# Separate PSUM tiles for the halves of the last TensorE conv tile, and one warm-up product fewer

## The chip, the cores and the metric

The kernel runs on one core of one Trainium2 chip. The metric is device time in microseconds (us) of one execution. Before the change it is 2915.72 us, the median of three runs (2914.89 to 2915.89).

## The reference

The input `x` is 16 images of 384 channels and 32 by 32 pixels, fp32. Two residual layers follow one another; each normalises in 32 groups of 12 channels first (`_gn`).

```python
# layer 0: attention over the 1024 pixels of an image, 8 heads of 48
x = x + _L0_conv_ref(_gn(x), L0_conv_w_qkv, L0_conv_w_proj, L0_conv_b_proj)
# layer 1: depthwise 7x7 convolution, weights made symmetric under rotation
x = x + _L1_conv_ref(_gn(x), L1_conv_weight)
```

`_L0_conv_ref` makes q, k and v with one product each, takes a softmax over 1024 keys, sums v with it and projects. `_L1_conv_ref` averages the weight with its three rotations by 90 degrees and convolves every channel with its own 49 taps.

## The kernel before

**Tiling.** An image is held as three tiles (k = 0, 1, 2) of 128 channels by 1024 pixels. `HALF` is 512 pixels, 16 of the 32 image rows. Heads are worked on in pairs. For a pair and eight blocks of keys, TensorE (PE) makes scores (`s_step`, L474), ScalarE (ACT) exponentiates them out of PSUM (L482), and PE sums v with them (`av_step`, L490).

**The start.** Image 0 is needed before anything else can run. While it is loaded, PE multiplies a tile of ones into a PSUM tile that nobody reads (`fill`, L1145). Then `groups_on_pe` makes the group means on PE with two short sets of products on masks (`average`, L313); between their results it calls `between`, which here is `fill(fills.popleft(), 2 * P)`: two products of 256 columns, then four (`fills = deque((2, 4))`). After the last set VectorE (DVE) and GpSimd (POOL) finish the scale (L332, L334, L335), and DVE, ACT and DVE normalise the three tiles of `x` (L341, L345, L341). The first product of q and k (`qk_step`, L423) is behind the fills in PE's queue.

**The convolution.** Most tiles are convolved on DVE, one `scalar_tensor_tensor` over the tile for each tap (`conv_tap`, L621). For three tiles, `PE_TILES` = (14, 2), (15, 2), (15, 1), PE does it (`conv_on_pe`, L729): each half of a tile is 14 taps (13 for the first tile) by four groups of 32 channels, 128 rows deep. A tile has one PSUM tile of two banks, `[P, 2, HALF]`, for both halves, from the pool `ps_s` with its three buffers. When a tile is finished, ACT copies it out (`conv_on_pe_end`, L744) and a transfer adds it to the residual. The last tile is instead added by DVE, half by half, and each half goes to the output at once (`conv_on_pe_half`, L752 and L753: half 0 by POOL's queue, half 1 by SP's).

**The last tile on DVE.** Tile (15, 0), `LONE`, has its 7 taps in the middle column done by ACT and added up in a tile `sum3` by POOL's transfers (L914). DVE does the other 42 taps in turns into two sums, the tile itself (`x` in the trace) and `sum2` (`sum` in the trace). Then it adds `sum3` to `sum2` (L888) and `sum2` to the tile in two halves (L894), each with an output transfer (L895, SP's and ACT's queues).

**The order.** Each engine works through its queue in the order in which the Python code emits instructions. A planner sets that order: `clock` is a model of PE's time, `vclock` one of DVE's. `conv_piece` emits seven taps of PE's convolution and adds 6.2 to `clock`; `catch_up(clock)` then emits DVE's work until `vclock` gets there, at `(950 + 128) / 955` = 1.129 for a tap of the last tile. Between taps it emits what `after(wait, cost, f)` has put on a list, as soon as `vclock` has reached the due time, which is `wait` behind the later of the two clocks at the call. Both halves of the last tile are put there with `after(6.0, 0.7, ...)`. A last tile half has two pieces, so 12.4 of `clock`.

**PSUM.** `ps_s` has three buffers of two banks. `ps_o` has two buffers of one bank (tag `acc`), which hold the sums of `av_step` and, in the last stage, the sums of the softmax (`ps_sum`) and the group means (`ps_st`).

Of the kernel before, what the change touches and what calls it, by code (L numbers as in the profile page):

```python
# [10 lines left out]
F32 = mybir.dt.float32  # L11
I32 = mybir.dt.int32
AF = mybir.ActivationFunctionType
ALU = mybir.AluOpType
AX = mybir.AxisListType

P = 128
# [27 lines left out]
def kernel(  # L45
# [25 lines left out]
    nc = tc.nc  # L71

    B, C, H, W = x.shape
# [5 lines left out]
    HALF = N // 2  # L79
# [30 lines left out]
    def run(general):  # L110
        tag = "g" if general else "f"
        with ExitStack() as stack:
# [3 lines left out]
            def pool(name, bufs, **kw):  # L116
                return stack.enter_context(tc.tile_pool(name=f"{name}_{tag}", bufs=bufs, **kw))
# [13 lines left out]
            ps_o = pool("ps_o", 2, space=bass.MemoryType.PSUM)  # L131

            def psum(name):
                return ps_s.tile([P, 2, HALF], F32, tag="s", name=name)

            xns, x1s, qks, os_, accs, es, xn1s = {}, {}, {}, {}, {}, {}, {}
            xds, shs, pss, mats, psums = {}, {}, {}, {}, {}
            PE_K = [NK - 1, NK - 2]

            PE_TILES = [(B - 2, PE_K[0])] + [(B - 1, k) for k in PE_K]  # L140
# [469 lines left out]
            def region(*ds):  # L610
                return [(slice(max(0, -d), H - max(0, d)), slice(max(0, d), H - max(0, -d))) for d in ds]
# [26 lines left out]
            SH, CH = 4, P // 4  # L638
# [77 lines left out]
            def pe_taps(b, k):  # L716
                return [t for t in PE_TAPS if t != (1, 0) or (b, k) not in ROWS_ONLY]

            def conv_on_pe(b, k, h, first, last):
                if (b, k) not in pss:  # L720
                    pss[b, k] = psum(f"ps_conv_{b}_{k}")
                taps = pe_taps(b, k)
                for n, (d0, dx) in enumerate(taps):
                    if not first <= n < last:
                        continue
                    _, (ox, ix) = region(0, dx)
                    for i in range(SH):
                        src = shs[b, k, h, i // 2][:, i % 2, 0 : ROWS * W]
                        nc.tensor.matmul(  # L729
                            pss[b, k][CH * i : CH * (i + 1), h, :].rearrange(  # L730
                                "p (y x) -> p y x", x=W
                            )[:, :, ox],
                            lhsT=mats[k][:, i, d0 * KS + dx + PAD, :],
                            rhs=src.rearrange("p (y x) -> p y x", x=W)[
                                :, SH * d0 : SH * d0 + H // 2, ix
                            ],
                            start=(n == 0),
                            stop=(n == len(taps) - 1),
                        )

            def conv_on_pe_end(b, k):

                t = tpool.tile([P, N], F32, tag="t", name=f"conv_{b}_{k}")
                nc.scalar.copy(t, flat(pss.pop((b, k))))  # L744
                nc.gpsimd.dma_start(x1s[b, k], t, accum_op=ALU.add)
                conv_end(b, k)

            def conv_on_pe_half(b, k, h):

                c = slice(h * HALF, (h + 1) * HALF)  # L750
                dst = x1s[b, k][:, c]
                nc.vector.tensor_tensor(dst, pss[b, k][:, h, :], dst, ALU.add)  # L752
                (nc.gpsimd, nc.sync)[h].dma_start(  # L753
                    out[b, k * P : (k + 1) * P].rearrange("p h w -> p (h w)")[:, c], dst
                )
# [88 lines left out]
            def now():  # L844
                return vclock if catching else max(clock, vclock)

            def after(wait, cost, f):

                nonlocal count
                count += 1  # L850
                heapq.heappush(later, (now() + wait, count, cost, f))
# [286 lines left out]
            ones = tpool.tile([P, N], F32, tag="t", name="ones_warm")[:, 0:HALF]  # L1138
            nc.vector.memset(ones, 1.0)
            warm = psum("warm")  # L1140
            fills = deque((2, 4))

            def fill(n, cols):
                for i in range(n):
# [60 lines left out]
            def loads(n):  # L1205
                while n and pe_loads and pe_loads[0][0] in xn1s:
                    (b, k), h, a = pe_loads.popleft()
                    conv_load(b, k, h, a)
                    n -= 1

            def conv_piece():
                nonlocal clock
                b, k, h, first, last = pe_conv.popleft()
                while (b, k, h, 1) not in shs and pe_loads:
                    loads(1)
                conv_on_pe(b, k, h, first, last)
                clock += 6.2 * (last - first) / KS
                if last == len(pe_taps(b, k)):
                    loads(2)
                    if (b, k) == PE_TILES[-1]:  # L1220
                        after(6.0, 0.7, lambda: conv_on_pe_half(b, k, h))
                    elif h == 1:
                        after(6.0, 1.2, lambda: conv_on_pe_end(b, k))

# [30 lines left out]
            def fast_end(b):  # L1255
                assert not applies
                for key in ("sum2", "sum3"):
                    late[key] = opool.tile([P, N], F32, tag="o", name=key)
                nc.gpsimd.memset(late["sum3"][:, N - W :], 0.0)

                x1_stats[b].groups_on_pe(late["masks"], tap, conv_piece)
                conv_piece()
                x1_chains(b, x1_stats[b])
# [7 lines left out]
            for b, n0, size in [  # L1271
# [27 lines left out]
                for n in range(n0, n0 + size):  # L1299
                    av_step(n)  # L1300
                    u, h, i = n // (2 * NT), n // NT % 2, n % NT
# [39 lines left out]


            conv_piece()
            fast_end(B - 1)
            clock += 7.0
            vclock = clock
            after(4.0, 1.2, check_vector)
            while later or chains or active or pe_conv:
# [6 lines left out]
                catch_up(clock)  # L1355

    run(False)
    redo = nc.values_load(again[0:1, 0:1], min_val=0, max_val=2 * P)
    with tc.If(redo > 0):
        run(True)  # L1360
# [43 lines left out]
```

## Time and profile before

| | |
|---|---|
| time, median of three runs | 2915.72 us |
| the profiled execution's own time | 2915.74 us |
| its span in the trace | 2913.9 us |
| PE busy | 2898.2 us (99%) |
| DVE busy | 2573.5 us (88%) |
| ACT busy | 1450.9 us (50%) |
| POOL busy | 258.0 us (9%) |
| mean granted clock of PE | 0.997 of full speed |

Times in the trace are counted from the start of the span. The 1.8 us between span and time lie outside the trace. A PE product in fp32 is two records in the trace, each with a weight load (PEld). DVE's and ACT's starts can lie some 0.08 us before the end of the instruction ahead, so the pitch from start to start is what an instruction takes in a row of others. A line of the timeline may merge several instructions of one kind: start, busy time, engine and line, and the count after an x. Square brackets hold idle time of the engine ahead of it, and what ended it.

### The profile page before, as it was taken

To read this page: it belongs to the slowest core of one execution; us is meant where nothing else is said; L and a number is where in the kernel's file an instruction comes from. 1 tells how busy PE (TensorE), PEld (TensorE's weight loads), DVE (VectorE), ACT (ScalarE), POOL (GpSimd) and SP (SyncE) were. 2 spreads that over 40 slices of the span, in tenths; PEclk is the share of its full clock that TensorE was granted. 3 is DMA by queue.
4 is the path that set the end of the run, shared out by engine and by line. 5 is a ranking of instruction groups with operands and counts; after the bars stand their busy time and mean duration, and the time that the engine had idled before them with its cause. 6 is when DMAs were issued, how large, how long until landed. Compare 5 with 4: busy or idle time off the path is not lost. (4 is left out here: it accounts for less than half of the span.)

```text
span 2913.9 us, 30140 instructions
## 1 busy us (share of the span) xinstructions
PE 2898.2 (99%) x11448; PEld 1168.7 (40%) x11448; DVE 2573.5 (88%) x2567; ACT 1450.9 (50%) x1732; POOL 258.0 (9%) x407
## 2 busy tenths in 40 slices
PE   9999999999999999999999999999999999999998
PEld 5343343433434343343433434343343433434332
DVE  5312998989899898998989899898998989899998
ACT  2545545465453655545465453655545465454531
POOL 3111004010100101000010100101001010100101
PEclk9999999999999999999999999999999999999999
DMA  7432012120312203022120312203012120312326
GB/s 282 133 28 63 16 35 76 35 70 17 67 37 43 70 21 84 16 35 70 35 70 16 66 39 43 70 21 84 16 35 70 33 72 16 64 41 43 98 62 180
DMA packets 73355, 172.84 MB, mean 59 GB/s; under 512 B 30432, under 2 KB 32368, under 8 KB 71664
## 3 DMA queue, kind: packets, MB, share of 16 engines
q0 software_dynamic: 33696, 112.73, 15.4%
q1 hardware_dynamic: 38080, 55.20, 7.8%
q10 hardware_dynamic: 1424, 2.88, 0.4%
q8 instruction: 92, 1.51, 0.2%
q14 instruction: 63, 0.52, 0.1%
HBM read 118.61 MB, written 28.72 MB: 51 GB/s over the span
## 5 line engine op out<-in xcount | busy, mean ns | idle before, releaser
L621 DVE SCALAR_TENSOR_TENSOR x<-xn,wsym,x 128x899 f32<-128x899 f32 (+9 forms) x2177 | 2370.4, 1162 | 139.6 <-ACT xn L345 139.6
L482 ACT ACTIVATE e<-ps_s 128x1024 f32<-128x1024 f32 x1024 | 952.4, 1053 | 54.5 <-PE ps_s L474 51.5
L474 PE MATMUL ps_s<-qk 48*128 48x512 f32 x4096 | 914.8, 596 | 1.4 <-ACT qk L430 1.4
L490 PE MATMUL acc<-e,v 128*64 128x512 f32 x4096 | 907.2, 595 | 0.0
L474 PEld LDWEIGHTS ps_s<-qk 48*128 48x128 f32 x4096 | 375.9, 185 | 536.5 <-ACT e L482 258.8
L490 PEld LDWEIGHTS acc<-e,v 128*64 128x64 f32 x4096 | 283.0, 137 | 608.2 <-issue 599.7
L423 PE MATMUL ps_qk<-x,wqk 128*128 128x512 f32 x1152 | 506.6, 596 | 0.0
L501 ACT COPY o<-acc 128x512 f32<-128x512 f32 x128 | 75.1, 587 | 609.4 <-PE acc L490 609.3
L423 PEld LDWEIGHTS ps_qk<-x,wqk 128*128 128x128 f32 x1152 | 216.8, 190 | 286.5 <-issue 286.3
L449 PE MATMUL ps_v<-wv,x 128*128 128x384 f32 x768 | 252.0, 488 | 0.0
L543 PE MATMUL ps_proj<-o,wp 128*128 128x512 f32 x540 | 234.2, 592 | 0.0
L430 ACT COPY qk<-ps_qk 128x1024 f32<-128x1024 f32 x96 | 96.7, 1009 | 254.0 <-PE ps_qk L423 254.0
L558 POOL DMA_DIRECT2D x<-in_x x45 | 39.3, 873 | 1794.7 <-ACT x L551 1421.0
L449 PEld LDWEIGHTS ps_v<-wv,x 128*128 128x128 f32 x768 | 144.6, 190 | 109.6 <-ACT e L482 12.1
L543 PEld LDWEIGHTS ps_proj<-o,wp 128*128 128x128 f32 x540 | 102.6, 190 | 125.9 <-issue 119.8
L458 ACT COPY v<-ps_v 128x384 f32<-128x384 f32 x128 | 55.1, 483 | 185.6 <-PE ps_v L449 185.6
L551 ACT ACTIVATE x<-ps_proj,bp 128x1024 f32<-128x1024 f32 x45 | 50.1, 1113 | 182.7 <-PE ps_proj L543 182.7
L526 DVE TENSOR_TENSOR o<-o,inv 128x1024 f32<-128x1024 f32 x63 | 76.8, 1219 | 68.0 <-DMA inv<-inv 62.6
L345 ACT ACTIVATE xn<-x,sc_x 128x1024 f32<-128x1024 f32 x47 | 54.9, 1230 | 90.1 <-DMA sc_x<-gr_x 66.9
L368 DVE BATCH_NORM_STATS2 bs_all<-xs 128x6 f32<-128x512 f32 x84 | 52.1, 683 | 17.7 <-DMA xs<-in_x 17.7
L729 PE MATMUL ps_conv<-sh,mat 128*32 128x464 f32 (+3 forms) x656 | 67.3, 569 | 0.0
L439 POOL DMA_DIRECT2D qk<-qk x96 | 47.3, 526 | 117.4 <-ACT qk L430 116.4
(135 smaller groups left out, 551.2 us busy)
## 6 DMA issues: line engine op xcount, KB each, us to landing
x<-in_x POOLq DMA_DIRECT2D x90, 512.0 KB, 5.6
inv<-inv SPq DMA_DIRECT2D x126, 256.0 KB
out<-x POOLq DMA_DIRECT2D x46, 512.0 KB, 3.9
xs<-in_x POOLq DMA_DIRECT2D x42, 512.0 KB, 6.5
qk<-qk POOLq DMA_DIRECT2D x96, 128.0 KB, 5.9
o<-o SPq DMA_DIRECT2D x90, 64.0 KB
sh<-xd SPq DMA_DIRECT2D x32, 160.0 KB
x<-in_x SPq DMA_DIRECT2D x6, 512.0 KB
```

Source lines behind the costliest of these rows:

```text
L423: nc.tensor.matmul(ps[:, h, :], lhsT=wqk[:, k, s, t, :], rhs=xns[b][:, k, h * HALF : (h + 1) * HALF], start=(k == 0), stop=(k == NK - 1),)
L430: nc.scalar.copy(halves(qks[u][:, s, :]), ps)
L449: nc.tensor.matmul(ps[:, j, 0:C], lhsT=xns[b][:, k, t * P : (t + 1) * P], rhs=wv[:, k, :], start=(k == 0), stop=(k == NK - 1),)
L458: nc.scalar.copy(dst.rearrange("p (h d) -> p h d", d=D + 1)[:, :, 0:D], ps[:, j, 0:C].rearrange("p (h d) -> p h d", d=D),)
L474: nc.tensor.matmul(ps[:, j, :], lhsT=qks[u][r, 1, i * P : (i + 1) * P], rhs=qks[u][r, 0, h * HALF : (h + 1) * HALF], start=True, stop=True,)
L482: nc.scalar.activation(es[n], ps, AF.Exp, scale=SCALE)
L490: nc.tensor.matmul(accs[u, h][64 * j : 64 * j + 64, :], lhsT=v_of(u, i, j), rhs=e[:, j, :], start=(i == 0), stop=(i == NT - 1),)
L501: nc.scalar.copy(os_[u][:, h * HALF : (h + 1) * HALF], accs.pop((u, h)))
L526: nc.vector.tensor_tensor(os_[u], os_[u], invs.pop(u), ALU.mult)
L543: nc.tensor.matmul(ps[:, h, :], lhsT=wp[:, t, o * P : (o + 1) * P], rhs=os_[NP * b + t][:, h * HALF : (h + 1) * HALF], start=(t == 0), sto ...
L621: nc.vector.scalar_tensor_tensor(acc, xn1s[b, k].rearrange("p (h w) -> p h w", w=W)[:, iy, ix], wsym[:, k, dy + PAD, dx + PAD : dx + PAD + 1],
L729: nc.tensor.matmul(pss[b, k][CH * i : CH * (i + 1), h, :].rearrange("p (y x) -> p y x", x=W)[:, :, ox], lhsT=mats[k][:, i, d0 * KS + dx + ...
```

## The change

1. In `conv_on_pe`, the last tile of `PE_TILES`, (15, 1), gets a PSUM tile of one bank for each half, from the pool `ps_o`. The other two tiles keep their tile of two banks.
2. `conv_on_pe_half` reads the half's own tile.
3. The halves' addition is put on the planner's list with `after(2.0, ...)` in place of `after(6.0, ...)`.
4. The second set of warm-up products ahead of the first q and k has three products in place of four.

```diff
             def conv_on_pe(b, k, h, first, last):
-                if (b, k) not in pss:
-                    pss[b, k] = psum(f"ps_conv_{b}_{k}")
+                if (b, k) == PE_TILES[-1]:
+
+                    if (b, k, h) not in pss:
+                        pss[b, k, h] = ps_o.tile([P, HALF], F32, tag="acc", name=f"ps_conv_{h}")
+                    dst = pss[b, k, h]
+                else:
+                    if (b, k) not in pss:
+                        pss[b, k] = psum(f"ps_conv_{b}_{k}")
+                    dst = pss[b, k][:, h, :]
...
-                            pss[b, k][CH * i : CH * (i + 1), h, :].rearrange(
-                                "p (y x) -> p y x", x=W
-                            )[:, :, ox],
+                            dst[CH * i : CH * (i + 1), :].rearrange("p (y x) -> p y x", x=W)[:, :, ox],
...
-                nc.vector.tensor_tensor(dst, pss[b, k][:, h, :], dst, ALU.add)
+                nc.vector.tensor_tensor(dst, pss.pop((b, k, h)), dst, ALU.add)
...
-            fills = deque((2, 4))
+            fills = deque((2, 3))
...
                     if (b, k) == PE_TILES[-1]:
-                        after(6.0, 0.7, lambda: conv_on_pe_half(b, k, h))
+                        after(2.0, 0.7, lambda: conv_on_pe_half(b, k, h))
```

## The prediction

> **What bounds the kernel now.** I read the page's busy times first, then the timeline of both ends, since the change touches only the first 20 us and the last 20.
>
> ```profile
> PE 2898.2 (99%) x11448; PEld 1168.7 (40%) x11448; DVE 2573.5 (88%) x2567; ACT 1450.9 (50%) x1732; POOL 258.0 (9%) x407
> ```
>
> PE lacks 15.7 us of the span: 1.46 before its first product, 1.10 before the first scores (from the waits of the first 31 us), and 12.8 at the end. Between the ends it has no gap, so what shortens its head moves everything behind it.
>
> The end, in the timeline:
>
> ```profile
> 2855.35 45.72 PE L729 MATMUL ps_conv<-sh,mat 128*32 128x512 f32 x445
> ...
> 2892.41 1.11 DVE L621 SCALAR_TENSOR_TENSOR sum<-xn,wsym,sum 128x870 f32<-128x870 f32 x1
> 2893.44 1.08 DVE L621 SCALAR_TENSOR_TENSOR x<-xn,wsym,x 128x841 f32<-128x841 f32 x1
> 2894.45 1.11 DVE L621 SCALAR_TENSOR_TENSOR sum<-xn,wsym,sum 128x870 f32<-128x870 f32 x1
> 2895.48 1.14 DVE L621 SCALAR_TENSOR_TENSOR x<-xn,wsym,x 128x899 f32<-128x899 f32 x1
> 2898.37 0.56 POOL L631 DMA_DIRECT2D out<-x  x1 [7.06 <-DMA x<-conv]
> 2901.16 0.69 DVE L752 TENSOR_TENSOR x<-ps_conv,x 128x512 f32<-128x512 f32 x1 [4.54 <-PE ps_conv L729]
> 2901.77 1.15 DVE L621 SCALAR_TENSOR_TENSOR sum<-xn,wsym,sum 128x899 f32<-128x899 f32 x1
> 2902.15 0.56 POOL L753 DMA_DIRECT2D out<-x  x1 [3.22 <-DVE x L752]
> ...
> 2905.05 1.23 DVE L888 TENSOR_TENSOR sum<-sum,sum 128x1024 f32<-128x1024 f32 x1
> ...
> 2907.51 0.68 DVE L752 TENSOR_TENSOR x<-ps_conv,x 128x512 f32<-128x512 f32 x1
> ...
> 2908.22 0.36 SPq L753 DMA_DIRECT2D out<-x  x1
> ```
>
> The first L752 adds half 0. DVE stood 4.54 us for it, and started 0.09 us after PE's very last product (2855.35 + 45.72 = 2901.07). When was half 0 done? The last two tiles are 448 records (2 tiles x 2 halves x 14 taps x 4 groups x 2), from 2855.31 to 2901.07: 0.102 us each. Half 1 is the last 112 of them, 11.4 us, so half 0 was complete at about 2889.6, 11.5 us before DVE might read it. The wait is for the whole tile. It also sets the end: from 2901.16 DVE has three taps, L888, L894 twice and half 1, without a gap, and half 1's output leaves at 2908.22; the span ends 5.7 later.
>
> The head, from the timelines of PE and its weight loads, and the table of 1 us stretches (columns: stretch, then busy us of PE, PEld, DVE, ACT, POOL, then PE's clock):
>
> ```profile
> 14.14 3.76 PE L1145 MATMUL warm<-ones_warm 128*128 128x256 f32 x8
> 17.70 4.63 PE L423 MATMUL ps_qk<-x,wqk 128*128 128x512 f32 x8
> ...
> 15.75 1.56 DVE L341 TENSOR_SCALAR x<-x,sc_x 128x1024 f32<-128x1024 f32 x2
> ...
> 18.00:19.00 1.00, 1.00 (x2) 0.37 (x2) 0.48 (x3) 0.00 (x0) 0.99 (x2) 0.50 0.99 393
> 19.00:20.00 1.00, 1.00 (x2) 0.34 (x1) 0.51 (x1) 0.00 (x0) 0.00 (x0) 0.62 0.98 397
> 20.00:21.00 1.00, 1.00 (x4) 0.51 (x3) 1.00 (x3) 0.00 (x0) 0.00 (x0) 1.00 0.64 229
> ```
>
> Four fills take 17.70 - 14.14 = 3.56 us, 0.89 each, at half clock. The first tile of `x` is ready at about 15.75 + 0.82 = 16.57 (the line holds two instructions, median 820 ns), so the fills, not the data, hold the first q and k. The clock becomes full at about 19.8 (0.62 over that stretch is 0.76 us at half and 0.24 at full).
>
> **What the Trainium skill says.** "PSUM — Partial Sum Buffer", Specifications (TRN2): a bank is 2 KiB per partition, 512 fp32 values. So the halves lie in banks of their own already; the summary of rules there asks a reader beside a running product only for another bank. The trace has that pair: ACT reads one score tile while PE writes the next. The 4.54 us is thus nothing that the memory asks for. "TensorE: Matmul & The Clock Gate", What's actually happening: the clock is raised after a busy window of some 3.4 us, and windows run freely. The trace agrees: clock at half from 13 to 19.8 us, two such windows. So one product fewer at 17 us should not delay the raise, as q and k products fill its place. "Perfetto Trace Analysis", Summary: the profiler window per engine type: the record of a transfer from SP's queue leaves out its data movement; hence the 5.7 us from issue to end of span, which I carry over unchanged.
>
> **The change part by part.**
>
> *Own tiles for the halves.* Nothing is computed more: 112 products go to other banks. Half 0 then needs only its own last product, at 2889.6. The two `acc` buffers were last read by DVE for `ps_sum` and for `ps_st` (L335 at 2842.78), 36 us before (15, 1) begins at about 2878.2; so no new wait on PE. `ps_s` loses one user, and no gap of PE there waited for it. Cost 0.
>
> *Where half 0 stands in DVE's queue.* Call C the model clock when half 0's last piece is emitted. Then half 1's first piece is emitted (C + 6.2) and DVE is filled up to there. With 6.0, half 0 was due at C + 6.0, but taps of 1.129 stepped over it, and it came out in the next fill, behind half 1's second piece; the trace agrees, as it stands after the tap of 2895.48. With 2.0 it comes out at the first step at or past C + 2.0, three or four taps earlier: at 2892.41 (taking four), 2.8 us after half 0 is done. No stall; DVE's 4.54 us goes. In numbers: the tap of 2895.48 is 899 wide; such a tap has a pitch of 2902.83 - 2901.77 = 1.06 (the next tap's start from the trace), so half 0 could have started at 2896.54 and did at 2901.16: 4.62 us. The 0.61 of half 0 itself only changes places with four taps.
>
> *Half 1.* It is due 2.0 behind C + 12.4, so at C + 14.4. Half 0 leaves at C + 2.0 to 3.13; with 0.7 for it and nine steps of 1.129 (seven taps, L888, L894) DVE's tile ends at C + 12.9 to 14.0. So half 1 stays last. It would start at 2907.51 - 4.62 = 2902.89, still 1.8 after PE's end; PE does not become the bound.
>
> *What is late next.* L888 moves to 2900.43 and needs `sum3`: its last add was issued at 2889.56 and took 4.3 to land (the list of transfers), 2893.9. Half 0's output on POOL's queue is behind L631, which waits until 2898.37 for the residual of (15, 2): so it leaves at about 2898.9 and not at 2893, 3.2 earlier than before, lands some 2.5 later, as measured, and is 2 us gone before L895 and half 1 send theirs (2902.4 to 2903.6). If POOL's wait grew by some 4 us, they would collide: 256 KB at the 300 GB/s of these stretches, up to 0.9.
>
> *One fill fewer.* PE gets to q and k 0.89 earlier, at 16.81; `x` at 16.57 plus a weight load at half clock (0.34) makes 16.9 the other limit. So 0.8 of q and k products are done earlier, but at half clock: worth 0.4 of full-clock time, as the raise at 19.8 stays. Bounds: 0 (raise already done in a run whose windows lie otherwise, and `x` the limit), 0.45 (0.89 halved). If the raise came one window later it would cost 3.4 x 0.5 = 1.7 (an estimate from the skill's window). I take 0.42. PE carries it to the end without a gap, and DVE's last stage hangs on PE's group means (L313), so the 0.42 adds to the 4.62.
>
> Sum: 5.04. The profiled execution, 2915.74, becomes 2910.7; the median, 2915.72, is the same. That is 0.17%, under the 0.2% (5.8 us) that I take as what a measurement can tell from no change.
>
> **The rivals.**
>
> *A, the gain is 5.0: 2910.7.* As above.
>
> *B, the wait moves along: 2919.4, slower.* If half 0 still waits for PE's last product (PE's progress reported only at the end of an unbroken run of products), the stall begins four taps earlier. Those taps, 2896.54 - 2892.41 = 4.13, then run after 2901: +4.13 - 0.42 = +3.7. It decides at the place where half 0 starts: the end moves by that start less 2897.0. Against it: the ACT copy L744 of (15, 2) ran at 2880.21, soon after that tile's end (2855.31 + 224 x 0.102 = 2878.2), with PE amid (15, 1). For it: this wait's release was PE's very end.
>
> *C, the end is hidden elsewhere: 2913.* DVE ends early, but outputs collide with POOL's late ones, or `sum3` lands late, and half of the 4.6 is lost (2915.7 - 2.3 - 0.4). Speaks for it: L631's wait of 7.06 shows a transfer slow to land; against: the DMA share is near nothing at 2902 to 2903.
>
> *D, the clock falls back: 2912.4.* The tail's 4.62 less 1.7, plus 0.4 at most: the fill was needed for the raise. Against it: PE stays busy without it.
>
> **How the numbers follow.** A 0.85, B 0.04, C 0.06, D 0.05. A's own range is 2910.2 to 2911.6: head 0 to 0.45, and 0.5 either way, as far as the three runs lie apart. D and half of C take the range to 2912.5; below, 2909.7, where a longer wait than the profiled one is taken away. Faster than 2909.9 is the low edge of A, 0.08; slower than 2921.5 nearly nobody, beyond B with a further loss: 0.02; the rest, 0.90, is within 0.2%, though below the time before.
>
> **What would show it.** After the change: L752 of half 0 without a wait, at about 2892, among taps of L621; half 1 at 2902.5, its output at 2903.2, and a span of 2908.9. L1145 with six records from 14.14, the first L423 at 16.8 to 16.95, clock raised near 19.8. I am wrong if L752 has a wait left on PE, if L888 waits for a transfer, or if the last output takes more than 5.7 to the end.

## The result, and the profile after

The kernel with the change takes 2909.64 us, the median of 22 runs (2907.99 to 2912.76). The kernel before takes 2914.93 us (22 runs, 2912.14 to 2917.80, the three that were known among them). The ratio of the two kernels' runs is estimated at 0.9985, with a 95% interval of 0.9979 to 0.9990: 4.4 us less, between 2.9 and 6.1; the two medians lie 5.3 apart. That is a gain, and under the 0.2% that the prediction set as its bound. The forecast was 2910.7, with a range of 2909.7 to 2912.5, so the median lies just below the range. The profiled execution took 2909.63 with a span of 2907.8, so 1.8 us lie outside the trace, as before.

The busy times of the page after the change:

```profile
PE 2896.3 (100%) x11446; PEld 1174.6 (40%) x11446; DVE 2573.6 (89%) x2567; ACT 1451.6 (50%) x1732; POOL 258.4 (9%) x407
```

PE has two records fewer, the one warm-up product. Work is otherwise what it was; what changed is when it is done. The end, in the timeline after the change:

```profile
2852.87 45.98 PE L736 MATMUL ps_conv<-sh,mat 128*32 128x512 f32 x445
...
2889.92 0.67 DVE L757 TENSOR_TENSOR x<-ps_conv,x 128x512 f32<-128x512 f32 x1
2890.53 1.11 DVE L621 SCALAR_TENSOR_TENSOR sum<-xn,wsym,sum 128x870 f32<-128x870 f32 x1
...
2896.36 0.56 POOL L631 DMA_DIRECT2D out<-x  x1 [6.97 <-DMA x<-conv]
2896.91 0.56 POOL L758 DMA_DIRECT2D out<-x  x1
...
2900.40 0.68 DVE L757 TENSOR_TENSOR x<-ps_conv,x 128x512 f32<-128x512 f32 x1
2901.11 0.36 SPq L758 DMA_DIRECT2D out<-x  x1
```

L757 is the line that was L752. Half 0 is added at 2889.92 with no bracket behind it: DVE does not wait for it. It stands before the tap of 870 elements, four taps earlier than before, and 8.9 us before PE's last product ends (2852.87 + 45.98 = 2898.85). Half 1 starts at 2900.40, which is 1.55 after PE's end; before it was 6.44 after.

The head, in the timeline of PE and the table of 1 us stretches (the last columns are PE's clock, the DMA share and GB/s):

```profile
14.19 2.91 PE L1150 MATMUL warm<-ones_warm 128*128 128x256 f32 x6
16.89 5.57 PE L423 MATMUL ps_qk<-x,wqk 128*128 128x512 f32 x12
...
16.00:17.00 1.00, 1.00 (x4) 0.64 (x3) 1.00 (x2) 1.00 (x1) 1.00 (x3) 0.50 0.35 33
17.00:18.00 1.00, 1.00 (x3) 0.42 (x2) 0.97 (x3) 0.04 (x1) 1.00 (x3) 0.80 0.70 209
```

The first product of q and k stands at 16.89, where it was at 17.70. But the clock is full from about 17.4 (0.80 over a stretch is 0.4 us at half and 0.6 at full), not from 19.8.

Put piece by piece, the two profiled executions compare so (us):

| piece | before | after | difference |
|---|---|---|---|
| span's start to the first scores | 30.29 | 28.71 | -1.58 |
| first scores to PE's end | 2870.78 | 2870.14 | -0.64 |
| PE's end to the start of half 1's addition | 6.44 | 1.55 | -4.89 |
| half 1's addition to its output's issue | 0.71 | 0.71 | 0 |
| that issue to the end of the span | 5.7 | 6.7 | +1.0 |
| span | 2913.9 | 2907.8 | -6.1 |

The third row is the change's aim. The last row was not foreseen, and the first is larger than the 0.42 of the prediction. The experiments take these three in turn.

### The profile page after: what moved, and what is told of

It is laid out like the page before. It is cut to its first block, busy times and chain, and to the rows that moved or that the text cites. A ratio compares the mean times of both kernels' runs of the same rounds, so it can differ in the third digit from the quotient of the medians.

```text
span 2907.8 us, 30136 instructions
## 1 busy us (share of the span) xinstructions
PE 2896.3 (100%) x11446; PEld 1174.6 (40%) x11446; DVE 2573.6 (89%) x2567; ACT 1451.6 (50%) x1732; POOL 258.4 (9%) x407
```

## The experiments

A difference in us below is the ratio's distance from 1 times the median of the kernel before in the same group of runs (2914.1 to 2914.7); it has the ratio's interval. Single executions of one kernel spread over some 3 to 6 us here, so an interval is 3 to 5 us wide, and the traces carry what is smaller.

### The tail's parts, one at a time

**Own tiles alone.** The kernel before with the new tiles, `after(6.0, ...)` and four fills left as they were.

```diff
+                if (b, k) == PE_TILES[-1]:
+                    if (b, k, h) not in pss:
+                        pss[b, k, h] = ps_o.tile([P, HALF], F32, tag="acc", name=f"ps_conv_{h}")
+                    dst = pss[b, k, h]
...
-                nc.vector.tensor_tensor(dst, pss[b, k][:, h, :], dst, ALU.add)
+                nc.vector.tensor_tensor(dst, pss.pop((b, k, h)), dst, ALU.add)
```

> Own PSUM tiles for the two halves alone; the halves' due time stays at 6.0 and four warm-up products stay. Theory A (DVE waited for the whole tile, and the tile is all of it): half 0's addition keeps its old place in DVE's order, four taps later than in the changed kernel, and has no wait; half 1's addition starts about 1.8 us after PE's last product, against 6.4 before; the last output leaves 4.6 us earlier, time -4.6 us. Theory B (a wait on PE's last product, whatever the tile): half 0 still waits about 4.5 us, time unchanged. Theory E (the earlier place in DVE's order is what matters): -1 us or less.

Measured: 2911.01, ratio 0.9989 (0.9982 to 0.9996), 3.2 us less. DVE's timeline:

```profile
2894.84 1.14 DVE L621 SCALAR_TENSOR_TENSOR x<-xn,wsym,x 128x899 f32<-128x899 f32 x1
2895.91 0.67 DVE L757 TENSOR_TENSOR x<-ps_conv,x 128x512 f32<-128x512 f32 x1
...
2902.25 0.68 DVE L757 TENSOR_TENSOR x<-ps_conv,x 128x512 f32<-128x512 f32 x1
```

Half 0 stands at its old place, behind the tap of 899, and is added without a wait. PE ended at 2900.44, so half 1 starts 1.81 after it. The tiles alone remove the whole wait.

**The earlier place alone.** The kernel before, shared tile, four fills.

```diff
-                        after(6.0, 0.7, lambda: conv_on_pe_half(b, k, h))
+                        after(2.0, 0.7, lambda: conv_on_pe_half(b, k, h))
```

> Only the halves' due time goes from 6.0 to 2.0; both halves stay in one PSUM tile, four warm-up products. DVE then has half 0's addition four taps earlier, in program order between the two pieces of half 1. Theory A (the wait goes by the tile): it waits about 3.0 us, for the last product of half 1's first piece, 5.7 us after half 0 is done, and PE's second piece has to wait for this read, a gap of about 0.75 us on PE; half 1's addition starts 4.1 us after PE's end, time -1.6 us. If the wait went by the bank of the half: no wait, no gap, -4.6 us. Theory E (the place alone): -4.6 us. Rival B of the prediction (the stall moves to the earlier place and lasts until PE's last product): +4.1 us.

Measured: 2913.54, ratio 0.9995 (0.9987 to 1.0003), no difference shown. The timeline of DVE and PE:

```profile
2894.90 0.69 DVE L752 TENSOR_TENSOR x<-ps_conv,x 128x512 f32<-128x512 f32 x1 [3.48 <-PE ps_conv L729]
2895.65 5.83 PE L729 MATMUL ps_conv<-sh,mat 128*32 128x464 f32 x56 [0.78 <-DVE x L752]
```

With the shared tile, half 0 still waits, but for the product emitted last before it, the end of half 1's first piece: 56 records, half 1's second piece, are still to come. And PE then waits 0.78 for DVE to have read, before it may write half 1's second piece. In these runs a tile is waited for as a whole in both directions, up to what stands ahead in the order of the program. Half 1 starts at 2905.40, 3.92 after PE's end (2901.48), against 6.44: 2.5 us better there, of which PE's gap takes 0.8 back.

**Both, with four fills.** The change without its last line.

```diff
-            fills = deque((2, 3))
+            fills = deque((2, 4))
```

> Own tiles and due time 2.0, but four warm-up products: the whole change but for the head. Theory A: as own tiles alone, -4.6 us, with half 0 added at once four taps earlier. If half 0's earlier place is worth something of its own, more than own tiles alone; if the head carries a good part of the change's 5.3 us, clearly less than 4.6.

Measured: 2910.85, ratio 0.9987 (0.9981 to 0.9994), 3.8 us less. Half 1 starts 1.54 after PE's end (2897.53 and 2899.07). Against the tiles alone that is 0.27 better, which is less than two executions of one kernel differ by (1.55 and, in a second execution further down, 0.93). So the earlier place adds nothing that can be shown.

**The fill alone.** The kernel before with `deque((2, 3))`.

```diff
-            fills = deque((2, 4))
+            fills = deque((2, 3))
```

> Only the warm-up product is taken out; one PSUM tile and due time 6.0 as before. Theory A: PE begins q and k 0.75 to 0.89 us earlier at half clock, time -0.4 us, the 4.5 us wait at the end unchanged. Theory D (the product is needed for the clock): the clock is raised one window later, +1.3 us. If the changed kernel's gain lay in the head: -2 us or more.

Measured: 2913.57, ratio 1.0002 (0.9993 to 1.0010): no difference shown. The wait for half 0 is still there, 5.04 us, and PE's head, in the timeline of this kernel, is another than in the kernel before:

```profile
2897.97 0.69 DVE L752 TENSOR_TENSOR x<-ps_conv,x 128x512 f32<-128x512 f32 x1 [5.04 <-PE ps_conv L729]
...
13.33 1.54 PE L1145 MATMUL warm<-ones_warm 128*128 128x256 f32 x6
15.84 10.57 PE L423 MATMUL ps_qk<-x,wqk 128*128 128x512 f32 x24 [0.97 <-DVE x L341]
```

Six records take 1.54 us here, 0.26 each, where those of the kernel before took 0.45: the clock was full throughout. PE is then done with the fills before `x` is, and waits 0.97 for it. The execution with both tail parts and four fills also had the full clock, and waits too:

```profile
13.19 1.97 PE L1150 MATMUL warm<-ones_warm 128*128 128x256 f32 x8
15.70 10.57 PE L423 MATMUL ps_qk<-x,wqk 128*128 128x512 f32 x24 [0.54 <-DVE x L341]
```

So in an execution with the full clock the fourth product stands wholly in the time in which PE waits for `x`, and taking it away changes only the length of the wait.

### Outputs late on POOL's queue?

The last row of the table above, 1.0 us more from the last issue to the end, had a first suspect: half 0's output stands behind L631 (512 KB, out at 2896.36) on POOL's queue, and took 5.3 us to land, where it was 2.5 before. This is rival C of the prediction: late bytes of POOL's would hold up the last outputs.

**POOL's outputs earlier.** The residual of (15, 2) is asked for sooner, and the last transfer into `sum3` later, so that L631 does not wait as long.

```diff
-                    due += 8.0
+                    due += 8.0 if len(adds) > 1 else 16.0
...
-                        after(6.0, 1.2, lambda: conv_on_pe_end(b, k))
+                        after(6.0 if b < B - 1 else 1.0, 1.2, lambda: conv_on_pe_end(b, k))
```

> The changed kernel, with POOL's queue in another order: the addition of PE's tile (15, 2) to the residual and its 512 KB output come ahead of the last addition to sum3 and not behind it, so they leave about 8 us earlier and POOL's queue is free when half 0 is done. In the kernels with own tiles the span ended 6.7 us after the last output was issued, with one shared tile 5.7. Theory T (POOL's two late outputs, 768 KB, are still moving or being confirmed when the last three outputs come): the 6.7 goes back to about 5.7, time 1.0 us under the changed kernel, -6 us against before. Rival U (the extra 1.0 belongs to the own tiles or to DVE's earlier end, not to transfers): 6.7 stays, time as the changed kernel. A loss if the last addition to sum3 now lands after 2896.7 and holds DVE's L893.

Measured: 2909.31, ratio 0.9984 (0.9977 to 0.9990), as the change itself. The timeline of the queues:

```profile
2891.21 0.56 POOL L631 DMA_DIRECT2D out<-x  x1 [8.88 <-DMA x<-conv]
2892.30 0.92 POOL L758 DMA_DIRECT2D out<-x  x1
2902.17 0.36 SPq L758 DMA_DIRECT2D out<-x  x1
```

Both outputs of POOL leave about 10 us before the last one, and the end (span 2908.7) still comes 6.5 after it. So late outputs of POOL's are not what makes the 5.7 into 6.7.

**Half 0's output on SP's queue.**

```diff
-                (nc.gpsimd, nc.sync)[h].dma_start(
+                nc.sync.dma_start(
```

> The changed kernel, with half 0's 256 KB output sent by SP's queue as soon as half 0 is added (about 2890.6), not by POOL's queue behind the 512 KB output that waits until 2896.4. Theory T: 256 of the 768 KB late bytes are gone, so the 6.7 us from the last issue to the end falls part of the way, to about 6.0 to 6.4; if the early transfer slows the addition of (15, 2) to the residual, POOL's 512 KB leaves up to 0.9 us later and the gain is lost. Rival U: 6.7 stays.

Measured: 2909.17, ratio 0.9984 (0.9978 to 0.9991). Half 0's output left at 2891.47; the end came 7.1 after the last issue (2901.96; span 2909.1). Had POOL's late bytes been the cause, 6.0 to 6.4 was expected.

### The head: none and eight fills

```diff
-            fills = deque((2, 3))
+            fills = deque((2, 0))
```

> The changed kernel without any warm-up product in the second set (0 in place of 3). Theory A: the first q and k then waits for x alone (L341, about 0.4 us earlier than the changed kernel's 16.9 at most), and PE does nothing for 2.4 us before, so the clock is raised one window later in most executions: 0 to +1.5 us against the changed kernel, -5 to -3 us against before. Rival D (even one product fewer costs the clock): fill_only would have shown it already, and here +1.7 and more. Rival H (every warm-up product costs about 1 us, as the medians of the changed kernel and of the one with four products suggest): -2 us or more against the changed kernel.

Measured: 2911.47, ratio 0.9993 (0.9985 to 1.0001). Against the two kernels of the last section, which ran beside it at 0.9984 and whose head is the change's, that is 2.6 us worse, though the intervals overlap (theirs reach 0.9990 and 0.9991). PE's timeline, and the stretches:

```profile
15.72 2.93 PE L423 MATMUL ps_qk<-x,wqk 128*128 128x512 f32 x3 [2.38 <-DVE x L341]
...
16.00:17.00 1.00, 1.00 (x2) 0.48 (x3) 0.96 (x3) 0.06 (x1) 1.00 (x2) 0.50 0.57 193
18.00:19.00 1.00, 1.00 (x3) 0.32 (x2) 0.49 (x1) 0.00 (x0) 0.06 (x1) 0.72 0.97 397
```

PE starts q and k early, at 15.72, after standing still for 2.38, but its clock falls to half at 15.2 and is full again only at about 18.6; the 24 records took 11.97 us and not the 10.57 of full clock. This execution's first scores, at 28.79, are no later than those of the change's first execution (28.71). So the trace shows the clock falling while PE stands still, and that leaving out the whole second set costs time is said by the run times alone.

```diff
-            fills = deque((2, 3))
+            fills = deque((2, 8))
```

> The changed kernel with 8 warm-up products in the second set in place of 3. Theory A: five more products in front of q and k, each worth 0.43 us of full-clock time (0.89 at half clock, half of which comes back since the clock is raised at the same time): +2.2 us against the changed kernel, -3 us against before. Rival H (about 1 us each): +5 us, the time of before.

Measured: 2911.95, ratio 0.9992 (0.9983 to 1.0000), 2.3 us worse than the same two, with intervals that overlap. The fills hold q and k up here:

```profile
14.23 5.38 PE L1150 MATMUL warm<-ones_warm 128*128 128x256 f32 x16
19.45 1.02 PE L423 MATMUL ps_qk<-x,wqk 128*128 128x512 f32 x2
```

### What lies between the last output and the end

The traces fall into two groups. From the last output's issue to the end it takes 5.7 with the kernel before, the earlier place alone and the fill alone; with every kernel so far whose half 0 has its own tile it takes 6.5 to 7.1. In the first group PE's last product ends 4.6 to 7.2 us ahead of the last issue, in the second 1.1 to 2.5 us ahead.

When an engine is done, it jumps past a second copy of the program that stands behind the first in the code and isn't run. The instructions of the line of this jump, in the kernel before (COMPARE_BRANCH is the jump, EVENT_SEMAPHORE waits for a counter or sets it; engine's queue, operation, count, duration in ns three times, then the first and last start in us):

```profile
L1359 SPq EVENT_SEMAPHORE  x8: 17/17/17, 2911.7 to 2912.2; - x8
L1359 PEldq COMPARE_BRANCH  x1: 4615/4615/4615, 2899.1 to 2899.1; - x1
...
L1359 PEldq EVENT_SEMAPHORE  x1: 51/51/51, 2903.8 to 2903.8; - x1
...
L1359 SPq COMPARE_BRANCH  x1: 50/50/50, 2908.6 to 2908.6; - x1
```

And after the change:

```profile
L1364 SPq EVENT_SEMAPHORE  x8: 17/17/17, 2905.6 to 2906.1; - x8
L1364 PEldq COMPARE_BRANCH  x1: 4370/4370/4370, 2896.7 to 2896.7; - x1
...
L1364 PEldq EVENT_SEMAPHORE  x1: 51/51/51, 2901.1 to 2901.1; - x1
...
L1364 SPq COMPARE_BRANCH  x1: 50/50/50, 2901.5 to 2901.5; - x1
```

SP's first instruction after its jump comes 3.1 us behind the jump before and 4.1 after (2908.6 to 2911.7, 2901.5 to 2905.6). That is the whole 1.0. But SP's first instructions behind the jump wait for the outputs to have landed, so a slower landing is a rival. By the semaphores in the traces the last output lands 3.3 us after its issue in the first group, and 4.0 to 4.6 in the second. In the changed kernel it lands at 2905.15, 0.4 ahead of SP's first instruction, so there the jump is what comes last. In the second execution of the change and in the kernel with wide products (both further down) it lands 0.3 to 0.4 us behind that instruction, so there the output comes last. Both have become slower, and which of the two comes last differs.

PE has its own jump behind it at 2903.8 before, 4.4 us ahead of the last issue (2908.22), and at 2901.1 after, at the very time of the last issue (2901.11). The Trainium skill, "Runtime: NRT & Kernel Launch", Instruction fetch mechanics, says that a jump out of the fetched pages forces a transfer of the target page before execution can go on. The trace agrees as far as it shows: there are queues of kind "instruction". These are the transfers from the last issue to the end, after the change (packets, MB, share of the engines):

```profile
q1 hardware_dynamic: 231, 0.41, 16.6%
q10 hardware_dynamic: 144, 0.26, 10.4%
q14 instruction: 6, 0.05, 2.6%
q8 instruction: 1, 0.02, 1.1%
```

A fetch of 16 KB on q8 falls into this stretch; in the kernel before q8 has none there. In all of the first group the last fetch on q8 starts 1.65 us or more ahead of the last issue, in all of the second 0.8 to 1.9 us behind it. From this comes theory F: PE's fetch, when it meets the last outputs and SP's and ACT's own fetches, holds these up by about 1 us. Against it stands theory T, that the lateness of POOL's queue makes the difference. Three more runs try F: DVE's tail made longer, made shorter, and the change as it is once more.

**DVE longer by three additions.**

```diff
+                    extra = tpool.tile([P, N], F32, tag="t", name="extra")
+                    for _ in range(3):
+                        nc.vector.tensor_tensor(extra, dst, dst, ALU.add)
```

They stand ahead of L893, and go into a tile that nobody reads.

> The changed kernel with three additions more on DVE ahead of L893 (sum2 + sum2 into a tile that nobody reads, 1.26 us each): DVE ends 3.8 us later, PE as before. Theory F (the 6.7 us in place of 5.7 comes from PE's jump to the program's last block: PE now ends 2.2 us before the last output is issued, in place of 7, so its 16 KB of instructions are fetched while the last outputs move and SP and ACT wait for theirs): the interval from the last issue to the end goes back to 5.7, the span is 2.8 us longer than the changed kernel's for 3.8 us of work. Rival V (own tiles make the interval 6.7 in themselves): 6.7 stays, span +3.8.

Measured: 2912.82, ratio 0.9998 (0.9989 to 1.0007). DVE's and SP's timeline:

```profile
2897.11 3.74 DVE L895 TENSOR_TENSOR extra<-sum 128x1024 f32<-128x1024 f32 x3
...
2904.07 0.36 SPq L758 DMA_DIRECT2D out<-x  x1
```

The instructions of the jump:

```profile
L1367 SPq EVENT_SEMAPHORE  x8: 17/17/17, 2907.5 to 2908.0; - x8
...
L1367 PEldq EVENT_SEMAPHORE  x1: 51/51/51, 2900.5 to 2900.5; - x1
...
L1367 SPq COMPARE_BRANCH  x1: 50/50/50, 2904.5 to 2904.5; - x1
```

PE has jumped 3.5 us ahead of the last issue, SP's jump takes 3.0 again, no fetch on q8 is left in the stretch, and the end comes 5.7 after the issue (span 2909.7). The median is 2.9 us above that of the change run beside it, for 3.74 us of added work. The own tiles are still there. So the tiles in themselves don't cost the 1.0; it comes where PE's end and the last outputs lie close. POOL's outputs were issued well ahead here too, so this run alone doesn't part F from T; the one with POOL's outputs earlier does, for SP's jump took 3.9 in it.

**DVE shorter by two taps.** The last two taps of the tile (15, 0) are left out.

```diff
-                return [t for t in TAPS if t[1] or t[0] not in ROWS_ONLY.get((b, k), ())]
+                taps = [t for t in TAPS if t[1] or t[0] not in ROWS_ONLY.get((b, k), ())]
+                return taps[:-2] if (b, k) == LONE else taps
```

> The changed kernel without the last two of the 42 taps that DVE does of tile (15, 0); these two taps are left out of the result. DVE's work is 2.1 us shorter. If DVE still sets the end: last issue 2.1 us earlier. By the trace of the changed kernel, half 1 can start at most 1.5 us earlier, as PE ends then: half 1's addition gets a wait on PE, last issue 1.5 us earlier. Theory F: PE's instruction fetch then falls yet later against the last output, and the interval to the end stays at 6.7 or grows by up to 1.4, so of 2.1 us of work 0 to 1.5 us are gained.

Measured: 2909.72, ratio 0.9984 (0.9977 to 0.9991), no better than the change. DVE's and SP's timeline:

```profile
2899.06 0.69 DVE L758 TENSOR_TENSOR x<-ps_conv,x 128x512 f32<-128x512 f32 x1 [0.95 <-PE ps_conv L737]
2899.78 0.36 SPq L759 DMA_DIRECT2D out<-x  x1
```

Half 1 now waits 0.95 for PE, and the end comes 7.4 after the last issue (span 2907.2). But this is not F's story. SP's jump, from 2900.2 to 2903.2, took 3.0, although a fetch on q8 starts in its middle, at 2901.85, as one does in every kernel of the second group. So such a fetch does not by itself hold SP up, and F as it was put does not hold. What came last is seen in the instructions of the kernel's closing line (the longest DRAIN of POOL is the first of its three):

```profile
L1406 POOLq DRAIN  x3: 46/103/3335, 2903.0 to 2906.9; - x3
L1406 SPq DRAIN  x3: 7/7/13, 2904.5 to 2906.6; - x3
```

and in the same line of the changed kernel:

```profile
L1405 POOLq DRAIN  x3: 46/103/3335, 2903.5 to 2907.6; - x3
L1405 SPq DRAIN  x3: 7/7/13, 2906.9 to 2907.3; - x3
```

POOL drains for 3.3 us after its last transfers, and the engines meet only when it is done. With the two taps less that is at 2903.0 + 3.3 = 2906.3, 1.8 behind SP's first DRAIN. In the changed kernel it is at 2906.8, and SP is the later one by 0.1 to 0.2. With POOL's outputs earlier, POOL's long DRAIN began at 2900.0, far ahead. So T has a part after all: POOL's queue, late with half 0's output behind L631, is the next thing that ends the program, close behind SP. It takes over as soon as SP is earlier. A kernel with both POOL's outputs earlier and a shorter DVE tail wasn't tried.

**The change once more.** The same kernel, beside these.

> The changed kernel itself, to stand beside the next three on one chip. By its earlier runs -4.4 to -5.3 us against before; last output to the end of the span 6.7 us, and PE's 16 KB instruction fetch after the last output is issued.

Measured: 2909.92, ratio 0.9990 (0.9982 to 0.9998), 2.9 us less than before. This profiled execution kept the full clock from 4.6 us on, with q and k at 15.86 and the first scores at 27.53, where the first one had 28.71. Half 1 started 0.93 after PE's end, where the first had 1.55; from the last issue (2900.08) to the end (2906.7) it took 6.6.

**Group means with wide products.** In the executions with half clock and warm-up products, the clock fell at about 12.6 to 14.5 us, during or just behind the second set of products for the group means, whose right side is one column. This kernel makes them 84 columns wide, all alike, and reads the first of each; what is computed is the same.

```diff
-                                    ps[:, c0 + mo : c0 + mo + 1],
+                                    ps[:, (c0 + mo) * WIDE : (c0 + mo + 1) * WIDE],
...
-                                    rhs=src[:, ki : ki + 1],
+                                    rhs=src[:, ki : ki + 1].to_broadcast([P, WIDE]),
```

> The changed kernel with the products on masks (L313) 84 columns wide in place of 1 (all columns equal, the first is read), in both places where group means are made. Theory W (the half clock at 14 to 18 us comes from the masks' products, which leave the array all but idle for 4 us; wide ones keep it at work and hide behind their weight loads of 0.12 us): the clock stays full from 6 us on, the first q and k starts at about 15.8 as x is ready, takes 10.6 us, and the first scores begin at about 27.4 in place of 28.7 to 29.8: 1 to 2 us under the changed kernel. Rival X (the clock drops all the same): the times of the changed kernel, or up to 0.5 us more for longer products.

Measured: 2909.20 (2907.62 to 2910.57), ratio 0.9982 (0.9975 to 0.9988), 5.2 us less than before. PE's timeline and the stretches:

```profile
11.58 1.70 PE L315 MATMUL ps_st_x<-d_x,masks 128*128 128x84 f32 x14
13.12 1.50 PE L1152 MATMUL warm<-ones_warm 128*128 128x256 f32 x6
15.65 10.57 PE L425 MATMUL ps_qk<-x,wqk 128*128 128x512 f32 x24 [1.04 <-DVE x L343]
...
14.00:15.00 1.00, 0.61 (x3) 0.19 (x1) 0.41 (x2) 0.25 (x1) 1.00 (x2) 1.00 0.09 5
15.00:16.00 1.00, 0.35 (x1) 0.30 (x2) 1.00 (x2) 0.99 (x1) 1.00 (x3) 1.00 0.09 29
```

The second set of means takes 1.70 us, no more than the 1.72 that its products of one column take in the changed kernel. The clock is full throughout, although PE is busy 0.61 and 0.35 of these two stretches only, and `x` is the limit at 15.65. The first scores start at 27.32. One such execution doesn't part W from X, as five of the thirteen with products of one column kept the full clock too.

The run times say more. All 21 runs of this kernel have a mean granted clock of 0.999. Of the change's runs 8 of 22 have it in the first comparison and 2 of 13 in the one beside this kernel; they are the fast ones (2907.99 to 2909.12), and the four at 0.997 are slow (2912.10 to 2914.04). The mean is no pure reading of the head: it holds PE's last microseconds too, and two profiled executions with 3.4 us of half clock also have 0.999. The 21 runs have a standard deviation of 0.65; the change beside them has 1.56, the change in the first comparison 1.30, and the kernel with two taps less 0.97. So W is supported, not proven. The ratio is the lowest of all, but its interval overlaps that of the change, so a gain in time is not shown.

### The heads side by side

| profiled execution | fills | half clock, from and to | first scores |
|---|---|---|---|
| before | 4 | 12.9 to 19.8 | 30.29 |
| own tiles alone | 4 | 13.4 to 20.3 | 30.55 |
| earlier place alone | 4 | 12.6 to 19.4 | 30.13 |
| both, four fills | 4 | none | 27.37 |
| the change | 3 | 14.0 to 17.4 | 28.71 |
| POOL's outputs earlier | 3 | 12.7 to 19.6 | 29.77 |
| half 0 by SP | 3 | 14.5 to 17.9 | 29.03 |
| the fill alone | 3 | none | 27.51 |
| three additions more | 3 | none | 27.51 |
| two taps less | 3 | none | 27.53 |
| the change once more | 3 | none | 27.53 |
| wide products for the means | 3 | none | 27.32 |
| no fills in the second set | 0 | 15.2 to 18.6 | 28.79 |
| eight fills | 8 | 14.3 to 17.7 | 31.02 |

At full clock three and four fills give the same start, within 0.2. Half clock lasts 6.8 us in some executions and 3.4 in others. Of those with 6.8, the three with four fills start later by half of what their clock rises later (30.13 at 19.44, 30.29 at 19.75, 30.55 at 20.25). At the rise of 19.57 that the one with three fills has, this gives 30.19; it started at 29.77. So one product fewer is worth 0.42 us there, by an estimate that rests on one execution with three fills. Which clock an execution has differs between executions of the same kernel, as the two of the change show, and moves the start by 1.2 there and by up to 3.2 between kernels.

## Why the prediction was right

**The wait was for the whole tile: right.** Own tiles alone remove all of it. The wait of 3.48 with the earlier place alone, for a product of half 1, and PE's gap of 0.78 show how a shared tile is waited for. The Trainium skill, "PSUM — Partial Sum Buffer", Specifications (TRN2), puts the two halves into two banks, and no run here shows DVE or PE slowed when both work on their own bank.

**Half 0's place: right on where, and worth little.** It is four taps earlier, as taken. With own tiles, the old place would have done.

**Half 1 stays behind DVE's work, 1.8 after PE's end: 1.55, and 0.93 in the second execution.** The 4.62 measured 4.63 with the tiles alone (6.44 - 1.81) and 4.89 with the whole change.

**"5.7 from the issue to end of span, which I carry over unchanged": this step failed.** It was 6.7, and 6.5 to 7.4 in every kernel in which the last issue came 2.5 us or less after PE's end. I had named a last output that takes more than 5.7 as a sign that I am wrong, and the sign came. The term of the sum is +1.0, so the tail brings 4.89 - 1.0 = 3.9 in the trace and not 4.62; the times say 3.2 and 3.8 for the two kernels with own tiles and four fills. Rival C had a loss at the end, of 2.3, by outputs on POOL's queue or by `sum3`. The loss came, at less than half that size, with SP's jump and the landing of the last output: POOL's outputs 10 us ahead of the last issue leave it at 6.5. What slows the two is open. POOL was 0.1 to 0.2 short of setting the end itself.

**Half 0's output lands 2.5 later: 5.3.** It was behind the 512 KB of L631. It cost nothing in the change, but it is what makes POOL's end so late, and two taps less of DVE ran into it.

**The head, -0.42: right where the clock is at half, nothing where it is full.** q and k came to 16.89 from 17.70, 0.81 of the 0.89, as predicted (16.8 to 16.95). But the clock rose at about 17.4, not 19.8, which is no effect of the fill: with three fills it rose at 17.4, 17.9 and 19.6. The lower bound, 0, is what executions with the full clock have. Where half clock lasts as long as in the kernel before, the traces give the 0.42 that was summed, from one execution with three fills. The times put the whole change 0.6 us ahead of the tail with four fills (0.9985 and 0.9987), which is far within their intervals, so they neither show nor refute it. The table's -1.58 and -0.64 hold more of the executions' own differences than of the change: first scores to PE's end lies between 2869.9 and 2870.6 in the first four experiments (with PE's gap of 0.78 taken off where it stands), with no change there.

**The rivals.** B, that the wait only moves along, is refuted for the change and half true for a shared tile. D is refuted for one product: with three fills no execution has half clock for longer than with four. For all of them the times speak for it, with intervals that overlap. A stands, with a tail 0.7 smaller than forecast and a median below A's own range of 2910.2 to 2911.6.

The forecast, 2910.7, is 1.1 above the median. That it is so near is luck in part, because errors of opposite sign stand against each other. The end's 1.0 was missed; half 1 gained 0.27 more than summed; the kernel before itself ran at 2914.93 beside the change, 0.8 below the three runs that were known; and the head's start is one of several that its executions have.

## What to carry to other kernels

Give each part of a result that is to be read by itself a tile of its own: two halves in one tile made the reader wait for the writer's whole stretch, 4.5 us, and, when the reader stood earlier in the order, made the writer wait for the reader too. When the engine that ends last is brought near to the end of another, the time from the last output to the end is not a constant: here it grew from 5.7 to 6.7, and a further 2.1 us taken from DVE went into a wait for PE and into POOL's closing, so look at every queue's last instructions, POOL's too. In a head that waits for data, look at the clock before counting products: one product was worth nothing at full clock and about 0.4 us at half, and with wide products for the means, which kept the mean clock of every run at 0.999, the runs spread less.

## What the runs showed of the hardware that was not expected

- A jump past the second copy of the program took SP 3.0 to 3.1 us where PE had jumped 2.4 us or more ahead of the last issue, and 3.8 to 4.5 where PE's jump ended from 0.2 ahead of it to 0.4 behind; PE's own jump took 3.7 to 4.8. With PE's jump 1.4 behind (two taps less), SP's took 3.0 once more, with a fetch on q8 in its middle. The last output's landing moved with the jump, from 3.3 us behind its issue to 4.0 to 4.6. That the engines' fetches and the outputs compete for transfer engines is argued from their lying close, and that q8 is PE's from its time; no run parts the fetch from its neighbours, so what delays SP stays open.
- POOL's closing DRAIN took 3.3 us in every kernel, wherever its last output stood, so an output on its queue has to land some 3 us sooner than one on SP's if it is not to be the last. In the changed kernel POOL's last output landed at 2902.25 and SP's at 2905.15, and POOL's closing was 0.1 to 0.2 short of being the last.
- Products with one column kept PE busy for 1.72 us per set by the trace, and yet the clock fell to half with them or just behind in most profiled executions. With 84 columns the sets took as long, and all 21 runs had a mean clock of 0.999 and spread less (0.65 against 0.97 to 1.56). That columns are what the clock goes by is argued.
- By the clock's record in the traces, the first rise at the start (the warm-up products then take half as long) came at 4.3 to 5.6 us in the six executions that kept the full clock, and at 5.8 to 7.7 in the seven with warm-up products that fell to half. So whether the clock falls goes with the moment of its first rise; the kernel without a second set, whose clock rose at 4.9 and fell while PE stood still, is the one exception. The execution with wide products had its rise at 4.9 too, within the stretch in which those of one column kept the full clock.
- PE waited for DVE's read of a half that it was not writing (0.78), because both halves were one tile.
